# A recommendation kernel's item stage: two of 32 gathered neighbours read as SBUF columns by ScalarE and VectorE, and a limit of two gathers in flight

## The chip, the cores and the metric

One core of a Trainium2 chip. The metric is the device time of one execution in microseconds (us); lower is better. The kernel before takes 31825.53 us, the median of 10 runs that lie between 31824.42 and 31826.89.

## The reference

Two stages. The item stage makes, for each of 50,001 items, an attention over its 32 neighbours in two embeddings of width 32. The user stage gathers, for each of 16,384 users, 100 history rows of width 128 and one target row, and ends in one number a user.

```python
def _neighbor_attn(E, near_full):                 # item stage, twice: E_in, E_out
    V = E[near_full]                              # [50001, 32, 32]
    scores = einsum('nd,nkd->nk', E, V) / sqrt(32)
    w = softmax(scores, axis=-1)
    return einsum('nk,nkd->nd', w, V)
...
h = concat([E_hist[history], a_sus[history], a_inf[history]])   # [16384, 100, 128]
t = concat([E_tgt[target], a_inf[target], a_sus[target]])       # [16384, 128]
z = relu(einsum('bld,hd->blh', h * t[:, None, :], W1) + b1)
exp_A = exp(einsum('blh,h->bl', z, W2[0])) * mask
result = h * (exp_A / sum(exp_A) ** 0.5)[..., None]
s = sum(result)                                   # one number for the whole batch
pred = cosine(s * ones, t);  return sigmoid(pred)
```

## The kernel before

Both embeddings lie side by side in one DRAM table, `egeo`, with 64 floats (256 B) a row, padded to 50,048 rows.

Item stage (L93 to L164). The items are cut into 23 iterations of 17 sub-tiles of 128 items: 391 sub-tiles. An iteration loads the neighbours' numbers `nidx`, its items' own rows `own` and the left half of `row` (L101 to L107). For a sub-tile, 32 indirect DMAs (L111), one for each neighbour, gather 128 rows of 256 B into `v`, one row to a partition; they are issued by GpSimd (POOL). Pool `n_v` has five buffers, so POOL can be up to five sub-tiles ahead. Then VectorE (DVE) multiplies by the item's own row (L120), sums to scores (L127), finds the maximum (L129, L130); ScalarE (ACT) makes the exponents (L134); DVE weighs the rows (L145, two halves), sums them (L152) and scales (L153) into `row`; ACT copies a swapped version into `trow` (L160). `own` and the exponents lie in PSUM when DVE reads them. At the end of an iteration SP's queue stores `row` to `table` and `trow` to `ttab` (L163, L164).

User stage (L176 to L292). For each of 128 blocks of 128 users, one indirect DMA gathers the targets' rows `t` from `ttab` (L197), and 100 gather the histories' rows `h` of 512 B from `table` (L233), four to a tile, with 12 tiles of `h`. PE transposes them (L246), DVE multiplies by the target and makes row sums (L248, L249), PE multiplies by W1 (L255), ACT applies the ReLU (L257), PE makes the scores (L265). Stages of three groups are interleaved. The user stage begins after the item stage's tables are stored.

The order of the instructions on each engine is the scheduler's; it also places the semaphore waits. Every indirect DMA tells of its landing by one of eight semaphores, taken in turn. At the start, ACT's queue issues a copy of 12.5 MB from `etgt` into `ttab` (L91, L92).

Of the kernel before, what the change touches and what calls it, by code (L numbers as in the profile page):

```python
# [9 lines left out]

F32 = mybir.dt.float32
I32 = mybir.dt.int32
AF = mybir.ActivationFunctionType
ALU = mybir.AluOpType
AX = mybir.AxisListType

P = 128
ITEMS = 50001
K = 32
G = 32  # L20
DE = 64
D = 128
# [7 lines left out]
NSUB = 17  # L30
NITER = -(-ITEMS // (P * NSUB))
ROWS = NITER * P * NSUB

# [7 lines left out]
def kernel(  # L43
# [11 lines left out]
    out: bass.AP,  # L55
):
    nc = tc.nc

    const = ctx.enter_context(tc.tile_pool(name="const", bufs=1))
    dram = ctx.enter_context(tc.tile_pool(name="dram", bufs=1, space=bass.MemoryType.DRAM))  # L60


    table = dram.tile([ROWS, D], F32, name="table")

    ttab = dram.tile([ROWS, D], F32, name="ttab")

    ident = const.tile([P, P], F32, name="ident")
# [16 lines left out]
    scale = 1.0 / math.sqrt(G)  # L84
    near_v = near.rearrange("(i p j) k -> i p j k", p=P, j=NSUB)
    egeo_v = egeo.rearrange("(i p j) d -> i p j d", p=P, j=NSUB)
    ehist_v = ehist.rearrange("(i p j) d -> i p j d", p=P, j=NSUB)
    table_v = table.rearrange("(i p j) d -> i p j d", p=P, j=NSUB)
    ttab_v = ttab.rearrange("(i p j) d -> i p j d", p=P, j=NSUB)

    nc.scalar.dma_start(ttab[0 : ITEMS - 1, 0:DE], etgt[0 : ITEMS - 1, :])  # L91
    nc.scalar.dma_start(ttab[ITEMS - 1 : ITEMS, 0:DE], etgt[ITEMS - 1 : ITEMS, :])  # L92
    with (  # L93
        tc.tile_pool(name="n_in", bufs=2) as n_in,
        tc.tile_pool(name="n_v", bufs=5) as n_v,
        tc.tile_pool(name="n_p", bufs=2) as n_p,
        tc.tile_pool(name="n_s", bufs=3) as n_s,
        tc.tile_pool(name="n_ps", bufs=2, space=bass.MemoryType.PSUM) as n_ps,
    ):
        for it in range(NITER):  # L100
            nidx = n_in.tile([P, NSUB, K], I32, name="nidx")  # L101
            nc.sync.dma_start(nidx, near_v[it])
            own = n_in.tile([P, NSUB, 2 * G], F32, name="own")
            nc.sync.dma_start(own, egeo_v[it])
            row = n_in.tile([P, NSUB, D], F32, name="row")
            nc.sync.dma_start(row[:, :, 0:DE], ehist_v[it])
            trow = n_in.tile([P, NSUB, 2 * G], F32, name="trow")  # L107
            for j in range(NSUB):
                v = n_v.tile([P, K, 2, G], F32, name="v")
                for k in range(K):  # L110
                    nc.gpsimd.indirect_dma_start(  # L111
                        out=v[:, k].rearrange("p t d -> p (t d)"),
                        out_offset=None,
                        in_=egeo,
                        in_offset=bass.IndirectOffsetOnAxis(ap=nidx[:, j, k : k + 1], axis=0),
                    )
                own_ps = n_ps.tile([P, 1, 2 * G], F32, name="own_ps")
                nc.scalar.copy(own_ps[:, 0, :], own[:, j, :])  # L118
                prod = n_p.tile([P, K, 2, G], F32, name="prod")
                nc.vector.tensor_tensor(  # L120
                    prod.rearrange("p k t d -> p k (t d)"),
                    v.rearrange("p k t d -> p k (t d)"),
                    own_ps.to_broadcast([P, K, 2 * G]),
                    ALU.mult,
                )
                sc = n_s.tile([P, 2, K], F32, name="sc")
                nc.vector.tensor_reduce(sc.rearrange("p t k -> p k t"), prod, AX.X, ALU.add)  # L127
                top = n_s.tile([P, 2], F32, name="top")
                nc.vector.tensor_reduce(top, sc, AX.X, ALU.max)  # L129
                nc.vector.tensor_scalar(top, top, -scale, None, ALU.mult)  # L130
                ex = n_ps.tile([P, 2, K], F32, name="ex")
                tot = n_s.tile([P, 2, 1], F32, name="tot")
                for t in range(2):
                    nc.scalar.activation(  # L134
                        ex[:, t, :],
                        sc[:, t, :],
                        AF.Exp,
                        bias=top[:, t : t + 1],
                        scale=scale,
                        accum_out=tot[:, t, :],  # L140
                    )
                nc.vector.reciprocal(tot, tot)  # L142
                wv = n_p.tile([P, 2, G, K], F32, name="wv")
                for t in range(2):
                    nc.vector.tensor_tensor(  # L145
                        wv[:, t].rearrange("p d k -> p k d"),
                        v[:, :, t, :],
                        ex[:, t, :].rearrange("p (k o) -> p k o", o=1).to_broadcast([P, K, G]),
                        ALU.mult,
                    )  # L150
                att = n_s.tile([P, 2, G], F32, name="att")
                nc.vector.tensor_reduce(att, wv, AX.X, ALU.add)  # L152
                nc.vector.tensor_tensor(  # L153
                    row[:, j, DE:D].rearrange("p (t d) -> p t d", t=2),
                    att,
                    tot.to_broadcast([P, 2, G]),
                    ALU.mult,
                )
                for t in range(2):
                    nc.scalar.copy(  # L160
                        trow[:, j, t * G : (t + 1) * G], row[:, j, D - (t + 1) * G : D - t * G]
                    )
            nc.sync.dma_start(table_v[it], row)  # L163
            nc.sync.dma_start(ttab_v[it][:, :, DE:D], trow)  # L164


    num = const.tile([P, UC], F32, name="num")
# [3 lines left out]
    hist_v = history.rearrange("(p i j) l -> i p j l", p=P, j=BSUB)  # L171
    tidx = const.tile([P, UC], I32, name="tidx")
    nc.scalar.dma_start(tidx, target.rearrange("(p c) -> p c", p=P))
    tidf = const.tile([P, UC], F32, name="tidf")
    nc.vector.tensor_copy(tidf, tidx)
    with (  # L176
# [12 lines left out]
        def target_rows(c):  # L189

            if c % BSUB == 0:
                hidx = u_in.tile([P, BSUB, L], I32, name="hidx")
                nc.sync.dma_start(hidx, hist_v[c // BSUB])
                hists[c // BSUB] = hidx

            t = u_t.tile([P, D], F32, name="t")
            nc.gpsimd.indirect_dma_start(  # L197
                out=t,
                out_offset=None,
                in_=ttab[0:ITEMS, :],  # L200
                in_offset=bass.IndirectOffsetOnAxis(ap=tidx[:, c : c + 1], axis=0),
            )
            users[c] = {"t": t, "hidx": hists[c // BSUB][:, c % BSUB, :]}

        def target_work(c):
# [8 lines left out]
            junk = u_t.tile([P, D], F32, name="junk")  # L214
            nc.scalar.activation(junk, t, AF.Square, accum_out=tsq[:, c : c + 1])
            idf = u_s.tile([P, L], F32, name="idf")
# [11 lines left out]
        def gather(c, g):  # L228
            u = users[c]
            h = u_h.tile([P, LG, D], F32, name="h")  # L230
            for q in range(LG):
                l = g * LG + q
                nc.gpsimd.indirect_dma_start(  # L233
                    out=h[:, q, :],
                    out_offset=None,
                    in_=table,
                    in_offset=bass.IndirectOffsetOnAxis(ap=u["hidx"][:, l : l + 1], axis=0),
                )
            u["h", g] = h

        def turn(c, g):
            u = users[c]
            h = u.pop(("h", g))
            hT_ps = ps_t.tile([P, LG, P], F32, name="hT_ps")
            for q in range(LG):
                nc.tensor.transpose(hT_ps[:, q, :], h[:, q, :], ident)  # L246
            xT = u_x.tile([D, LG, P], F32, name="xT")
            nc.vector.tensor_tensor(xT, hT_ps, u["tT"].to_broadcast([D, LG, P]), ALU.mult)  # L248
            nc.vector.tensor_reduce(u["hsum"][:, g * LG : (g + 1) * LG], h, AX.X, ALU.add)  # L249
            u["xT"][g] = xT  # L250

        def hidden(c, g):
# [3 lines left out]
            z = u_x.tile([HID, LG, P], F32, name="z")  # L256
            nc.scalar.activation(z, z_ps, AF.Relu, bias=b1_sb)  # L257
            u["z"][g] = z

        def scored(c, g):  # L260
# [9 lines left out]
            ea = u_s.tile([P, L], F32, name="ea")  # L270
            nc.scalar.activation(ea, u["score"], AF.Exp)
            nc.vector.tensor_tensor(ea, ea, u["keep"], ALU.mult)
# [7 lines left out]
        for s in range(len(groups) + 2):  # L280
            if s < len(groups):
                c, g = groups[s]
# [12 lines left out]
    with (  # L295
# [3 lines left out]
        root = f_s.tile([P, UC], F32, name="root")  # L299
        nc.scalar.activation(root, den, AF.Sqrt)  # L300
        part = f_s.tile([P, UC], F32, name="part")
# [6 lines left out]
        s = f_s.tile([P, 1], F32, name="s")  # L308
# [4 lines left out]
        nc.vector.tensor_scalar(n1, n1, float(D), EPS * EPS, ALU.mult, ALU.max)  # L313
        nc.scalar.activation(n1, n1, AF.Sqrt)
        n2 = f_s.tile([P, UC], F32, name="n2")
# [65 lines left out]
```

## Time and profile before

| what | value |
|---|---|
| median of 10 runs | 31825.53 us |
| the profiled execution | 31823.54 us, its span 31821.7 us |
| POOL busy | 24022.8 us (75%), 25446 instructions |
| PE busy | 15251.9 us (48%) |
| DVE busy | 8950.1 us (28%) |
| ACT busy | 2850.7 us (9%) |
| gathers of the item stage (L111) | 12512, 944 ns each |
| gathers of the user stage (L233, L197) | 12800 and 128, 944 ns each |
| first gather of the item stage, of the user stage | at 8.4 us, at 15654.1 us |

The page gives, for an engine, the time in which its instructions ran. Under the groups, each line has the busy time of a group, the mean of one instruction in ns, and the idle time of the engine just before these instructions with what ended it. "issue" means that the engine waited for nothing that the profile shows. An indirect DMA on POOL counts as busy while POOL makes its descriptors; the transfer itself goes on afterwards, and "landing" is the moment at which its semaphore is complete, counted from the instruction's start. The chain of waits follows the work that ended last back through what released it; each of its pieces has a start, a length and a name.

### The profile page before, as it was taken

Reading aid. Unit: us, or ns where it says so; the run is one execution under the profiler, and the core shown is the slowest. Engines: PE = TensorE matmul, PEld = TensorE weight load, DVE = VectorE, ACT = ScalarE, POOL = GpSimd, SP = SyncE. Lnnn points to the kernel's source line nnn. Section 1 sums busy time; section 2 is a strip of 40 time slices with the busy share of each in tenths; the row PEclk is TensorE's granted clock in tenths of the full one; section 3 lists DMA queues with packets and bytes.
Section 4 is the critical chain, followed back from the end, with each engine's and each line's share of the span. In section 5 each row is a group of like instructions: output and inputs, shape, how many; then the busy total and the mean of one; then the engine's idle time right before and its main releaser. Section 6 shows DMA issues by size and latency. Waiting matters only on the chain.

```text
span 31821.7 us, 154035 instructions
## 1 busy us (share of the span) xinstructions
PE 15251.9 (48%) x44931; PEld 9633.2 (30%) x44931; DVE 8950.1 (28%) x10957; ACT 2850.7 (9%) x6458; POOL 24022.8 (75%) x25446
## 2 busy tenths in 40 slices
PE   0000000000000000000299999999999999999999
PEld 0000000000000000000155555555555555555555
DVE  2222222222222222222222222222222222222222
ACT  0000000000000000000011111111111111111111
POOL 7777777777777777777777777777777777777777
PEclk9999999999999999999955555555555555555555
DMA  2111111111111111111122222222222222222221
GB/s 50 30 30 30 30 31 33 30 30 30 30 34 30 30 30 30 31 33 28 37 54 53 54 53 54 53 54 54 53 54 53 54 53 54 54 53 54 53 54 52
DMA packets 981065, 1358.75 MB, mean 43 GB/s; under 512 B 559873, under 2 KB 564353, under 8 KB 977281
## 3 DMA queue, kind: packets, MB, share of 16 engines
q0 software_dynamic: 814080, 1258.87, 17.0%
q1 hardware_dynamic: 115952, 77.16, 0.9%
q10 hardware_dynamic: 50192, 12.87, 0.2%
q8 instruction: 363, 5.95, 0.1%
q14 instruction: 478, 3.91, 0.0%
HBM read 1308.76 MB, written 51.30 MB: 43 GB/s over the span
## 4 chain that ended last, share of the span: by engine, by line
POOL 48%; issue 19%; PE 16%; DMA 13%; DVE 2%; ACT 1%; POOLq 0%; ACTq 0%; SPq 0%; DVEq 0%
POOL v L111 35%; POOL h L233 13%; DMA h<-table,hidx 11%; PE z_ps L255 8%; PE score L265 5%; PE hT_ps L246 3%; DMA v<-in_egeo_dram,nidx 2%; DVE xT L248 2%; ACT z L257 1%; POOL t L197 0%; POOLq L233 0%; DVE ea L274 0%; DVE tT L211 0%; DMA ttab<-trow 0%; DMA nidx<-in_near_dram 0%
## 5 line engine op out<-in xcount | busy, mean ns | idle before, releaser
L233 POOL DMA_INDIRECT h<-table,hidx x12800 | 12088.6, 944 | 3899.7 <-issue 3169.8
L111 POOL DMA_INDIRECT v<-in_egeo_dram,nidx x12512 | 11812.7, 944 | 3818.2 <-issue 3727.6
L209 PE MATMUL hT_ps<-ident,t 128*128 128x128 f32 x128 | 53.9, 421 | 15650.1 <-DMA t<-ttab,tidx 15650.1
L265 PEld LDWEIGHTS score<-w_sb,z 128*128 128x128 f32 x25600 | 6226.6, 334 | 1075.0 <-ACT z L257 1068.7
L255 PE MATMUL z_ps<-xT,w1T 128*128 128x512 f32 x6400 | 6529.5, 1124 | 0.0
L265 PE MATMUL score<-w_sb,z 128*128 128x1 f32 x25600 | 5906.4, 335 | 228.7 <-ACT z L257 150.7
L246 PE MATMUL hT_ps<-ident,h 128*128 128x128 f32 x12800 | 4724.1, 440 | 675.3 <-DMA h<-table,hidx 523.0
L249 DVE TENSOR_REDUCE hsum<-h 128x4 f32<-128x512 f32 x3200 | 2194.3, 686 | 9256.4 <-DMA h<-table,hidx 9239.4
L209 PEld LDWEIGHTS hT_ps<-ident,t 128*128 128x128 f32 x128 | 28.7, 224 | 15650.3 <-ACT idf L217 15650.3
L246 PEld LDWEIGHTS hT_ps<-ident,h 128*128 128x128 f32 x12800 | 2675.4, 209 | 5447.2 <-issue 3254.6
L120 DVE TENSOR_TENSOR prod<-v,own_ps 128x2048 f32<-128x2048 f32 x391 | 894.2, 2287 | 10800.5 <-DMA v<-in_egeo_dram,nidx 10800.2
L257 ACT ACTIVATE z<-z_ps,b_sb 128x512 f32<-128x512 f32 x3200 | 2198.7, 687 | 13456.8 <-PE z_ps L255 13345.8
L248 DVE TENSOR_TENSOR xT<-hT_ps,tT 128x512 f32<-128x512 f32 x3200 | 2209.7, 691 | 2026.7 <-PE hT_ps L246 2025.4
L255 PEld LDWEIGHTS z_ps<-xT,w1T 128*128 128x128 f32 x6400 | 1746.2, 333 | 0.0
L145 DVE TENSOR_TENSOR wv<-v,ex 128x1024 f32<-128x1024 f32 x782 | 1399.2, 1868 | 0.0
L118 ACT COPY own_ps<-own 128x64 f32<-128x64 f32 x391 | 84.4, 216 | 11505.2 <-DVE prod L120 11503.8
L127 DVE TENSOR_REDUCE sc<-prod 128x64 f32<-128x2048 f32 x391 | 894.5, 2288 | 13.5
L152 DVE TENSOR_REDUCE att<-wv 128x64 f32<-128x2048 f32 x391 | 893.7, 2286 | 13.4
L160 ACT COPY trow<-row 128x32 f32<-128x32 f32 x782 | 131.7, 215 | 2466.0 <-DVE row L153 2466.0
L134 ACT ACTIVATE ex<-sc,top 128x32 f32<-128x32 f32 x782 | 227.7, 291 | 1082.6 <-DVE top L130 1070.0
L142 DVE RECIPROCAL tot<-tot 128x2 f32<-128x2 f32 x391 | 64.8, 166 | 362.4 <-ACT ex L134 362.4
L197 POOL DMA_INDIRECT t<-ttab,tidx x128 | 120.8, 944 | 60.6 <-issue 60.6
(49 smaller groups left out, 808.9 us busy)
## 6 DMA issues: line engine op xcount, KB each, us to landing
h<-table,hidx POOLq DMA_INDIRECT x12800, 2.5
v<-in_egeo_dram,nidx POOLq DMA_INDIRECT x12512, 2.4
table<-row SPq DMA_DIRECT2D x23, 1088.0 KB, 4.4
own<-in_egeo_dram SPq DMA_DIRECT2D x23, 544.0 KB, 3.7
row<-in_ehist_dram SPq DMA_DIRECT2D x23, 544.0 KB, 6.8
ttab<-trow SPq DMA_DIRECT2D x23, 544.0 KB, 6.7
ttab<-in_etgt_dram ACTq DMA_DIRECT2D x1, 12500.0 KB, 52.2
hidx<-in_history_dram SPq DMA_DIRECT2D x32, 200.0 KB, 2.5
```

What stands on the lines that cost most here:

```text
L111: nc.gpsimd.indirect_dma_start(out=v[:, k].rearrange("p t d -> p (t d)"), out_offset=None, in_=egeo, in_offset=bass.IndirectOffsetOnAxis(a ...
L120: nc.vector.tensor_tensor(prod.rearrange("p k t d -> p k (t d)"), v.rearrange("p k t d -> p k (t d)"), own_ps.to_broadcast([P, K, 2 * G]), ...
L127: nc.vector.tensor_reduce(sc.rearrange("p t k -> p k t"), prod, AX.X, ALU.add)
L145: nc.vector.tensor_tensor(wv[:, t].rearrange("p d k -> p k d"), v[:, :, t, :], ex[:, t, :].rearrange("p (k o) -> p k o", o=1).to_broadcast ...
L152: nc.vector.tensor_reduce(att, wv, AX.X, ALU.add)
L233: nc.gpsimd.indirect_dma_start(out=h[:, q, :], out_offset=None, in_=table, in_offset=bass.IndirectOffsetOnAxis(ap=u["hidx"][:, l : l + 1], ...
L246: nc.tensor.transpose(hT_ps[:, q, :], h[:, q, :], ident)
L248: nc.vector.tensor_tensor(xT, hT_ps, u["tT"].to_broadcast([D, LG, P]), ALU.mult)
L249: nc.vector.tensor_reduce(u["hsum"][:, g * LG : (g + 1) * LG], h, AX.X, ALU.add)
L255: nc.tensor.matmul(z_ps, w1T, u["xT"].pop(g), start=True, stop=True)
L257: nc.scalar.activation(z, z_ps, AF.Relu, bias=b1_sb)
L265: nc.tensor.matmul(u["score"][:, l : l + 1], z[:, q, :], w2_sb, start=True, stop=True)
```

## The change

Three things change.

First, the item stage takes two of each item's 32 neighbours out of the gathers. At the start the whole table `egeo` is brought into SBUF in transposed form, `geoT`: 128 partitions by 25,024 columns of 4 bytes, where a column holds the 128 floats of two neighbouring rows (an even and an odd item). It is made by 66 loads on SP's queue (`transposed`), PE transposes and ACT copies. For an iteration, `load` works out the address of the column of each item's last two neighbours on DVE and transposes these addresses into one row for each sub-tile and neighbour (`cols`). For a sub-tile, ScalarE reads one neighbour and VectorE the other: each loads 128 addresses into registers, 32 at a time, and copies 128 columns of 4 bytes on each partition, one instruction to a column, into `g` (`columns`). PE transposes `g` back (`turn`), ACT copies the even item's half into `v` (`even`), and DVE overwrites it with the odd item's half where the number is odd (`odd_half`). The option of fetching a neighbour by single-row DMAs on SP's queue is in the code and switched off (`SPNUM` is 0).

Second, the order of the item stage on PE, ACT, DVE and SP is written out by hand: step s issues the gathers and columns of sub-tile s, the products, scores and exponents of s-1, the weighing and sums of s-2 and the last copies of s-3, with the column copies spread in eight portions between them. The stores of `row` and `trow` go to ACT's queue. `n_p` has one buffer instead of two.

Third, each indirect DMA of both stages goes through `gather_rows`, which makes it wait for the landing of the indirect DMA issued two before it (`AHEAD` is 2).

```diff
+AHEAD = 2
+AUX = ("AAAA", "DDDD",)
+NAUX = len(AUX)
+SPNUM, SPDEN = 0, 1
+NREG = 32
+PAIRS = ROWS // 2
+NST = 3
...
+    geoT = nc.alloc_sbuf_tensor("geoT", (P, PAIRS), F32).ap()
...
+    def gather_rows(**kw):
+        g = nc.gpsimd.indirect_dma_start(**kw)
+        if len(issued) >= AHEAD:
+            tc.add_manual_dep(g.ins, issued[-AHEAD].ins.name, landed, reason="AHEAD")
+        issued.append(g)
...
+        tc.manual_schedule(engines={E.PE, E.Activation, E.DVE, E.SP}),
+        tc.tile_pool(name="n_st", bufs=2) as n_st,
-        tc.tile_pool(name="n_p", bufs=2) as n_p,
+        tc.tile_pool(name="n_p", bufs=1) as n_p,
+        tc.tile_pool(name="n_g", bufs=2) as n_g,
...
+        def transposed(q):
...
+            nc.sync.dma_start(
+                st[0:h, 0:n, :],
+                egeo_p[base : base + h * n, :].rearrange("(p n) d -> p n d", n=n),
+            )
...
+                for r in range(m):
+                    nc.tensor.transpose(ps[:, r, 0:h], st[0:h, n0 + r, :], ident[0:h, 0:h])
+                if (n0 // 4) % 2:
+                    nc.vector.tensor_copy(into[:, n0 : n0 + m, :], ps[:, 0:m, 0:h])
+                else:
+                    nc.scalar.copy(into[:, n0 : n0 + m, :], ps[:, 0:m, 0:h])
...
+        def gather(s):
...
+            k1 = K - NAUX - 1
+            by_sp = s * SPNUM % SPDEN < SPNUM
...
+            for k in range(k1 if by_sp else k1 + 1):
+                gather_rows(
+                    out=v[:, k].rearrange("p t d -> p (t d)"),
...
+        def columns(s, a, i0):
+            e = AUX[a][i0 // NREG]
+            vals = registers(s, a + 1, ENGINE[e], i0, geoT_at, geoT_at + 4 * (PAIRS - 1))
+            g = subs[s]["g"][a].bitcast(U8)
+            copy = nc.scalar.copy if e == "A" else nc.vector.tensor_copy
+            for i in range(i0, i0 + NREG):
+                copy(g[:, 4 * i : 4 * i + 4], geoT_b[:, ds(vals[i - i0] - geoT_at, 4)])
+
+        def turn(s):
+            back = n_pt.tile([P, 4, P], F32, name="pt")
+            for a in range(NAUX):
+                nc.tensor.transpose(back[:, a, :], subs[s]["g"][a], ident)
...
+        def even(s):
+            nc.scalar.copy(subs[s]["aux"], subs[s]["back"][:, 0:NAUX, 0 : 2 * G])
...
+        def odd_half(s):
+            nc.vector.copy_predicated(
+                subs[s]["aux"],
...
+                subs[s]["back"][:, 0:NAUX, 2 * G : 4 * G],
+            )
...
-            nc.sync.dma_start(table_v[it], row)
-            nc.sync.dma_start(ttab_v[it][:, :, DE:D], trow)
+            if j == NSUB - 1:
+                nc.scalar.dma_start(table_v[it], row)
+                nc.scalar.dma_start(ttab_v[it][:, :, DE:D], trow)
...
+        for s in range(NT + 3):
+            if s < NT:
+                if s % NSUB == NSUB // 2 and s // NSUB + 1 < NITER:
+                    load(s // NSUB + 1)
+                gather(s)
+            one, two, three = (0 <= s - d < NT for d in (1, 2, 3))
+            work = [
+                lambda: one and turn(s - 1),
+                lambda: (two and weighted(s - 2, 0), one and even(s - 1)),
+                lambda: two and weighted(s - 2, 1),
+                lambda: one and (odd_half(s - 1), products(s - 1)),
+                lambda: one and scores(s - 1),
+                lambda: two and attend(s - 2),
+                lambda: three and finish(s - 3),
+                lambda: one and exponents(s - 1),
+            ]
+            for w in range(len(work)):
+                work[w]()
+                if s < NT:
+                    for blocks in (acts, dves):
+                        n = len(blocks)
+                        for c in blocks[-(-w * n // 8) : -(-(w + 1) * n // 8)]:
+                            columns(s, *c)
...
-            nc.gpsimd.indirect_dma_start(
+            gather_rows(
                 out=t,
...
-                nc.gpsimd.indirect_dma_start(
+                gather_rows(
                     out=h[:, q, :],
```

## The prediction

> **What bounds the kernel now.** I read the page's busy times first, then its groups, then the list of waits, then the chain of waits in small windows. Busy times alone mislead here: no engine is above 75%.
>
> ```profile
> PE 15251.9 (48%) x44931; PEld 9633.2 (30%) x44931; DVE 8950.1 (28%) x10957; ACT 2850.7 (9%) x6458; POOL 24022.8 (75%) x25446
> ...
> L233 POOL DMA_INDIRECT h<-table,hidx x12800 | 12088.6, 944 | 3899.7 <-issue 3169.8
> L111 POOL DMA_INDIRECT v<-in_egeo_dram,nidx x12512 | 11812.7, 944 | 3818.2 <-issue 3727.6
> ```
>
> The two gather groups hold 23,901 us of busy time and 7,718 us of idle time that nearly all ends by itself ("issue"): together almost the whole span. The order of time shows the same as a fixed beat:
>
> ```profile
> 199.66 0.94 POOL L111 DMA_INDIRECT v<-in_egeo_dram,nidx  x1 [0.30 <-issue]
> 200.90 0.94 POOL L111 DMA_INDIRECT v<-in_egeo_dram,nidx  x1 [0.30 <-DMA v<-in_egeo_dram,nidx]
> 202.15 0.94 POOL L111 DMA_INDIRECT v<-in_egeo_dram,nidx  x1 [0.30 <-issue]
> 203.40 0.94 POOL L111 DMA_INDIRECT v<-in_egeo_dram,nidx  x1 [0.30 <-issue]
> ```
>
> A gather takes 0.945 us and the next starts 0.30 us later: one per 1.249 us (202.15 to 203.40), in both stages. The item stage is 12,512 x 1.2487 = 15,624 us, the user stage (12,800 of h, 128 of t) 12,928 x 1.249 = 16,147 us, sum 31,771; the rest of the 31,821.7 us span is 8.4 us ahead of the first gather, 22 us between the stages and the tail. The profiled execution took 31,823.5 us, 2 us under the median of 31,825.5, so I add changes to 31,824.
>
> The second thing to read is how long a gather takes to land, since the change makes gathers wait for that. From the chain of waits in three windows (start, length, what):
>
> ```profile
> 2.19 5.96 DMA nidx<-in_near_dram
> 8.15 0.28 issue
> 8.43 1.10 POOL v L111
> ...
> 198.41 2.43 DMA v<-in_egeo_dram,nidx
> 200.83 0.02 issue
> 200.86 0.02 POOLq L111
> 200.87 0.03 issue
> 200.90 0.94 POOL v L111
> ...
> 15653.36 0.04 POOLq L197
> 15653.41 0.70 issue
> 15654.11 0.94 POOL t L197
> ```
>
> An item gather lands 2.43 us after it starts (others in that view 2.33 to 2.47). In the user stage, rows of twice the size land after 2.44 to 2.59, middle 2.50. Two beats are 2.50 us. So there are already hardly more than two gathers in flight, and the new limit falls on the very moment at which the next one starts today.
>
> **The change, part by part.**
>
> *Removed gathers.* 30 of 32 neighbours stay on POOL: 391 x 2 = 782 gathers less, 782 x 1.249 = 977 us less at today's beat. All of it is on the path.
>
> *The wait.* Gather n now waits for the landing of n-2, in both stages, for all 11,730 + 12,928 = 24,658. Behind a waiting gather stand all later gathers, which are all that POOL has to do; behind them DVE and PE. If X is the time from a landing to the start of the gather that waited for it, the beat is the larger of 1.249 and (landing + X)/2. X is the number on which all hangs. Rows bound it: 0.07 (200.83 to 200.90), 0.28 (8.15 to 8.43), 0.70 (15653.41 to 15654.11). I distrust the first: the list of waits gives 274 such waits in the item stage, all with a gap of 0.30 like the 12,237 gathers that waited for nothing; a wait that truly held the gather would scatter its start with the landing (2.33 to 2.47). There the sequencer was ahead, the next gather already handed over. The other two are starts of an idle POOL, and a gather released by a landing meets an idle POOL. I take 0.28, the one gather whose own wait ended with a landing; 0.70 also follows eight semaphore instructions in a row.
> Item: (2.43 + 0.28)/2 = 1.355, x 11,730 = 15,894, against 15,624: +270 us, the saving of 977 included.
> User: (2.50 + 0.28)/2 = 1.39, x 12,928 = 17,970, against 16,147: +1,823 us. Nothing is removed here; the wait is pure cost.
>
> *Slow landings.* Today a late landing costs nothing; with the wait it does. While the 12.5 MB copy into ttab runs, gathers land after 5.8 us (median from 8 to 51 us); around the stores of an iteration (699 to 712 us) the median is 4.7. At the boundaries some five gathers lose (4.7 - 2.43)/2 = 1.1 us, 23 times: 130 us. At the start the beat is (5.8 + 0.28)/2 = 3.0 for 43 us: 14 gathers instead of 34, 27 us. Estimate 140 together, as the start overlaps the next item.
>
> *The transposed table.* 66 loads of 196 KB, 198 transposes (0.44 us), 66 ACT copies of 128x384 (0.22 at 64 wide, 0.69 at 512: about 0.55). With two staging buffers, 2.7 us for a load (nidx, 272 KB) and one copy behind another, about 2.5 us a round, 165 us; ACT begins after 51 us, as its queue is held by the ttab copy (49.4 us). So the first columns come at about 220 us and the first v buffer is free two steps later, near 285. POOL fills five buffers (150 gathers) by about 240. Stall about 50 us, once. Sum so far 190 beside the two stages.
>
> *ScalarE's and VectorE's columns, hidden or not.* A sub-tile lasts 30 x 1.355 = 40.7 us on POOL. VectorE has 11.3 us of work today (2.29 + 2.29 + 3.58 + 2.29 and four of about 0.2), one predicated copy (0.3) and 128 small copies: 0.09 each if they follow as closely as the scaling after the 128x2 reciprocal (95.87 to 95.96), 0.166 if they last like it: 11.5 to 21.2. ScalarE has 1.8 us and 128 copies at 0.125 (two trow copies in 0.34) to 0.215: 16 to 27.5. Each also loads 128 registers, which no row shows: from a semaphore instruction of the sequencer (0.017) to a whole small VectorE instruction (0.166), 2 to 21 us. VectorE 25 to 54, ScalarE 20 to 50. I take the lower half, below 40.7, and cost it at nothing: POOL's gathers hide it. If VectorE were at 54, the item stage would be 391 x 54 = 21,114. The drain after the last gather grows by two sub-steps, some 10 us. Moving the stores of row and trow from SP's to ACT's queue is 46 issues of 0.3 to 0.6 us on an engine with slack: nothing.
>
> A rule of the Trainium skill speaks against the registers: "Runtime: NRT & Kernel Launch", section on instruction fetch, gives about 200 ns for each register that a sequencer loads, even in bulk. No row here shows a register load. By that rule 128 loads are 25.6 us, VectorE's step is an estimated 48.7 us, the item stage 19,040 and the whole 37,250.
>
> Second, does VectorE slow the gathers? Gathers are 940/945 ns (min/median) in a stretch with VectorE 28% busy, and the same in the user stage: not today. "SBUF — State Buffer", section "Who interferes with whom", says that a VectorE copy with both ends in SBUF can take the port pair that GpSimd needs and block it for a whole instruction; today's large operations are not of that kind, the 128 new copies may be. By it up to 128 x 0.166 = 21 us of a sub-tile could be blocked; no run here shows it, and I leave it out.
>
> Sum: 31,824 + 270 + 1,823 + 190 = 34,107: I say 34,100.
>
> **Rivals.**
> *Faster: the wait costs nothing.* If the sequencer passes a landing on within 0.07, as that row reads, item is 1.25 x 11,730 = 14,663 (-961), user 1.285 x 12,928 = 16,612 (+465); with 190 for start and slow landings 31,520. If it is hidden wholly, -977 + 190 gives 31,040. It decides at X = 0.09, where the two stages cancel. For it: the 200.90 row. Against: 0.30 in every one of them. That the limit isn't in force at all (no wait in the program) ends in the same place.
> *Slower by little: X = 0.12*, the time from a landing to VectorE's start (the last gather 87.26, landing 2.43 later, prod at 89.81): item 1.275 (-668), user 1.31 (+789), 190: 32,140.
> *Slower by much: the columns bind, or X is 0.70.* VectorE passes POOL's 40.7 us when a register costs over 0.137 us at the small spacing. At 54 us: 31,824 + 5,490 + 1,823 + 190 = 39,330. X = 0.70 gives item 1.565 (+2,733), user 1.60 (+4,538): 39,290. For it: nothing here shows a register load, and the one other idle start is long.
>
> **How the numbers follow.** X from 0.2 to 0.4 with the columns hidden, 0.47: 33,100 to 35,600, centre 34,100. Little slower, 0.14. Much slower, 0.20. Faster, 0.19 (31,000 to 31,700). A measurement here can tell 0.2% (64 us) from no change; only a narrow X near 0.09 falls within: 0.03, taken from faster and little slower. So faster 0.17, same 0.03, slower 0.80. The range runs from 31,000 (the free wait) to 36,500, leaving out most of the much-slower case and little else; the likeliest case's own range is 33,100 to 35,600.
>
> **What would show it.** POOL's gathers keep 945 ns, but the gap before them in both groups is put down to DMA instead of issue, with starts in pairs or a steady 1.36 (item) and 1.39 (user). Item stage about 15,900 us, user stage about 18,000. The user stage is the cleanest: only the wait changed there. Wrong: a user beat of 1.25 with gaps of 0.30 (the wait is free); a POOL that waits for v buffers released by VectorE or ScalarE (the columns bind); gathers longer than 945 ns (the port).

## The result and the profile after

The kernel after takes 36,628.68 us (median of 8 runs, 36,614.93 to 36,654.23), beside 31,825.83 us for the kernel before in the same comparison: 1.151 times as long, with a 95% interval of 1.150 to 1.152. The prediction was 34,100 us; the sign was right, the loss was 2.1 times the forecast (4,803 us instead of 2,274), and the time lies 129 us above the range.

The profiled execution took 36,628.49 us, its span 36,626.4. From the starts of the gathers in its trace: the first starts at 9.6 us, the item stage takes 16,506 us (11,730 gathers, 1.407 us each), 23 us lie between the stages, the user stage takes 20,069 us (12,928 gathers, 1.552 us each), the tail 18 us.

The page of the kernel after: busy time of each engine, then the shares of the chain that ended last, then four groups of instructions.

```profile
PE 16229.4 (44%) x45932; PEld 9562.5 (26%) x45932; DVE 12711.4 (35%) x61557; ACT 7855.2 (21%) x56963; POOL 23270.6 (64%) x24664
...
DMA 69%; issue 12%; PE 12%; DVE 2%; POOL 2%; ACT 2%; POOLq 0%; ACTq 0%; DVEq 0%; SPq 0%
...
L84 POOL DMA_INDIRECT h<-table,hidx x12800 | 12079.4, 944 | 7729.1 <-DMA h<-table,hidx 5736.1
L84 POOL DMA_INDIRECT v<-in_egeo_dram,nidx x11730 | 11069.8, 944 | 5444.9 <-DMA v<-in_egeo_dram,nidx 4876.0
...
L240 ACT COPY g<-geoT 128x4 uint8 x50048 | 4919.1, 189 | 2151.1 <-issue 2149.8
...
L240 DVE COPY g<-geoT 128x4 uint8 x50048 | 3847.7, 195 | 2252.8 <-issue 2135.3
```

A gather still holds POOL for 944 ns. What grew is the idle time before it: 5,444.9 us for `v` and 7,729.1 for `h`, where it was 3,818.2 and 3,899.7, and most of it now ends with a landing and not by itself. The chain is 69% DMA. VectorE and ScalarE carry 100,096 column copies, and neither stands in the chain with more than 2%.

In the order of time POOL's beat of 0.30 us gaps is gone. Start, length, instruction, and in brackets the gap before it with what ended it, in the user stage of the kernel after:

```profile
16749.07 0.94 POOL L84 DMA_INDIRECT h<-table,hidx  x1 [0.31 <-issue]
16750.69 0.95 POOL L84 DMA_INDIRECT h<-table,hidx  x1 [0.68 <-DMA h<-table,hidx]
16751.94 0.94 POOL L84 DMA_INDIRECT h<-table,hidx  x1 [0.30 <-DMA h<-table,hidx]
16753.92 0.94 POOL L84 DMA_INDIRECT h<-table,hidx  x1 [1.04 <-DMA h<-table,hidx]
16755.17 0.94 POOL L84 DMA_INDIRECT h<-table,hidx  x1 [0.31 <-issue]
```

Gathers now start in pairs, and the gaps ahead of the pairs differ: 0.68, then 1.04. The chain of waits around the same moment (start, length, what) tells the two apart:

```profile
16747.06 0.02 issue
16747.08 0.04 POOLq L84
16747.12 0.70 issue
16747.82 2.61 DMA h<-table,hidx
16750.43 0.26 issue
16750.69 2.47 DMA h<-table,hidx
16753.15 0.02 issue
16753.18 0.04 POOLq L84
16753.22 0.70 issue
16753.92 2.54 DMA h<-table,hidx
```

From a landing to the start of the gather that waited for it there are two prices, not one. Where the gather itself holds the wait it is 0.26 us (16750.43 to 16750.69). Where POOL's sequencer has a semaphore instruction ahead of the gather ("POOLq") it is 0.02 + 0.04 + 0.70 = 0.76 us (16753.15 to 16753.92). Over the whole trace the first is 0.259 us with hardly any scatter (least 0.258), the second 0.763 in the user stage, with 9 of 10 of the gathers that had to wait between 0.760 and 0.766. A tile that PE or VectorE gives back late would scatter it. Where two semaphore instructions stand ahead of a gather (39 times) the middle is 0.824, so the price goes with the instructions.

In the item stage the first price is the rule, with a third one now and then. The chain in a window there:

```profile
355.96 2.45 DMA v<-in_egeo_dram,nidx
358.41 0.26 issue
358.67 2.50 DMA v<-in_egeo_dram,nidx
361.17 1.74 issue
362.90 2.48 DMA v<-in_egeo_dram,nidx
```

The 1.74 us (358.67 + 2.50 to 362.90) returns at every 106th gather in the order of the program. It is plainest where every gather waits (e4 below): of the 233 gathers in that place, 201 started 1.73 to 1.74 us after the landing and 31, with a semaphore instruction ahead of them, some 3.34 us.

How often does a semaphore instruction stand ahead of a gather? The view of the gathers' line counts them (duration in ns, first and last start). The kernel after, user stage from 17,000 us on:

```profile
L84 POOLq EVENT_SEMAPHORE  x3280: 17/43/43, 17000.2 to 36596.3; - x193
```

and the kernel before, whole:

```profile
L233 POOLq EVENT_SEMAPHORE  x3219: 17/43/43, 15709.3 to 31790.0; - x190
```

About one for four gathers, in both: a tile of `h` holds four gathers, and the first of them waits for the tile to be free as well as for a landing. Before, it costs nothing: of 25,439 gaps between gathers only two are over 0.4 us, since the sequencer hands a gather over while POOL still works on the one before. After, 13,130 of 24,657 gaps are.

### The profile page after: what moved, and what is told of

It reads as the page before. It is cut to its first block, busy times and chain, and to the rows that moved or that the text cites. A ratio compares the mean times of both kernels' runs of the same rounds, so it can differ in the third digit from the quotient of the medians.

```text
span 36626.4 us, 262157 instructions
## 1 busy us (share of the span) xinstructions
PE 16229.4 (44%) x45932; PEld 9562.5 (26%) x45932; DVE 12711.4 (35%) x61557; ACT 7855.2 (21%) x56963; POOL 23270.6 (64%) x24664
## 4 chain that ended last, share of the span: by engine, by line
DMA 69%; issue 12%; PE 12%; DVE 2%; POOL 2%; ACT 2%; POOLq 0%; ACTq 0%; DVEq 0%; SPq 0%
DMA v<-in_egeo_dram,nidx 38%; DMA h<-table,hidx 31%; PE z_ps L461 6%; PE score L471 5%; DVE xT L454 2%; ACT z L463 2%; POOL v L84 2%; PE hT_ps L452 1%; POOL h L84 1%; DMA t<-ttab,tidx 0%; DVE hsum L455 0%; POOLq L84 0%; DVE ea L478 0%; ACT ea L477 0%; DVE den L479 0%
## 5 line engine op out<-in xcount | busy, mean ns | idle before, releaser
L84 POOL DMA_INDIRECT h<-table,hidx x12800 | 12079.4, 944 | 7729.1 <-DMA h<-table,hidx 5736.1
L84 POOL DMA_INDIRECT v<-in_egeo_dram,nidx x11730 | 11069.8, 944 | 5444.9 <-DMA v<-in_egeo_dram,nidx 4876.0
L461 PE MATMUL z_ps<-xT,w1T 128*128 128x512 f32 x6400 | 6451.9, 1112 | 1603.9 <-DVE xT L454 1599.4
L245 PE MATMUL pt<-ident,g 128*128 128x128 f32 x782 | 363.7, 471 | 15041.0 <-DVE g L240 9864.5
L471 PEld LDWEIGHTS score<-w_sb,z 128*128 128x128 f32 x25600 | 5715.2, 328 | 1617.6 <-ACT z L463 1550.5
L452 PE MATMUL hT_ps<-ident,h 128*128 128x128 f32 x12800 | 4963.6, 440 | 1931.0 <-DMA h<-table,hidx 1915.7
L240 ACT COPY g<-geoT 128x4 uint8 x50048 | 4919.1, 189 | 2151.1 <-issue 2149.8
L452 PEld LDWEIGHTS hT_ps<-ident,h 128*128 128x128 f32 x12800 | 2984.7, 246 | 6698.3 <-DMA h<-table,hidx 3734.5
L240 DVE COPY g<-geoT 128x4 uint8 x50048 | 3847.7, 195 | 2252.8 <-issue 2135.3
L245 PEld LDWEIGHTS pt<-ident,g 128*128 128x128 f32 x782 | 141.7, 183 | 15259.0 <-DVE g L240 9972.3
L251 ACT COPY v<-pt 128x128 f32<-128x128 f32 x391 | 104.0, 266 | 2487.0 <-PE pt L245 2475.8
```

Of the source, the lines that this page charges most:

```text
L84: g = nc.gpsimd.indirect_dma_start(**kw)
L240: copy(g[:, 4 * i : 4 * i + 4], geoT_b[:, ds(vals[i - i0] - geoT_at, 4)])
L461: nc.tensor.matmul(z_ps, w1T, u["xT"].pop(g), start=True, stop=True)
L471: nc.tensor.matmul(u["score"][:, l : l + 1], z[:, q, :], w2_sb, start=True, stop=True)
```

## The experiments

The runs were made in three batches, on the chips numbered 3, 0 and 2; which one the result came from is not on record. So each stands beside the kernel before on its own chip, which took 36,292 us in the first batch (seven runs, 36,284 to 36,298) and 31,809 us in the second and third. Where the landings can be read there, their medians are a little shorter (2.37 us item, 2.46 us user, beside 2.44 and 2.52 in the kernel after's first trace).

### First batch: no limit, the limit alone, three, one

**e1_no_limit.** The columns without the limit.

```diff
-AHEAD = 2
+AHEAD = 10**9
```

> The changed kernel with AHEAD at 10**9, so that no gather waits for an earlier one; the columns stay. Theory (the wait is the whole loss: a gather released by a landing starts 0.26 us after it, because the sequencer can no longer hand it over early; the columns are hidden): both stages fall back to one gather per 1.249 us. Item stage 11,730 x 1.249 = 14,650 us and up to 60 us of a late start, user stage 16,150, the whole 30,850 to 30,950: faster than before by 2.8%. Rival A (the columns on ScalarE and VectorE hold POOL back, by late buffers or by the port that VectorE and POOL share): the item stage stays above 15,624, gathers longer than 945 ns or waits of POOL for v buffers, the whole above 31,825. Rival B (the user stage suffers from something else in the change): its beat stays above 1.30, the whole above 32,000.

Measured: 38,956.76 us, ratio 1.073 (1.072 to 1.075) against 36,292. If the limit alone were the cause, this kernel would have been faster than the one before; here it is slower. Page groups of this kernel:

```profile
L84 POOL DMA_INDIRECT v<-in_egeo_dram,nidx x11730 | 11100.0, 946 | 8974.5 <-DVE wv L305 5505.7
L84 POOL DMA_INDIRECT h<-table,hidx x12800 | 12107.6, 946 | 6433.5 <-issue 3584.7
L240 ACT COPY g<-geoT 128x4 uint8 x50048 | 5869.5, 190 | 11021.0 <-issue 10783.9
...
L240 DVE COPY g<-geoT 128x4 uint8 x50048 | 4609.3, 184 | 8173.8 <-issue 7933.6
```

POOL waited for VectorE to release `v`, once a sub-tile, and the column copies were slow not in themselves (184 and 190 ns) but in the time between them. VectorE in order of time:

```profile
8042.48 0.17 DVE L240 COPY g<-geoT 128x4 uint8 x1 [1.22 <-issue]
8043.88 0.17 DVE L240 COPY g<-geoT 128x4 uint8 x1 [1.23 <-issue]
```

1.40 us from copy to copy, put down to nothing that the profile shows. The kernel before was 14% slower on this chip as well. So this run says something about the chip and nothing yet about the limit; it was made again below.

**e2_limit_alone.** The kernel before, with all three indirect DMAs through the same `gather_rows`; no columns.

```diff
-                nc.gpsimd.indirect_dma_start(
+                gather_rows(
```

> The kernel before with the limit of two gathers in flight alone; no columns. Theory: item beat as in the changed kernel, 1.41, x 12,512 = 17,640; user beat 1.552, x 12,928 = 20,070; with 55 for start, gap and end 37,760, some 1,130 over the changed kernel, which is the 782 gathers more at 1.41 and little else. Rival A (part of the changed kernel's item beat comes from the columns): an item beat nearer 1.35, the item stage 16,900, the whole about 37,000.

Measured: 36,799.14 us, ratio 1.014 (1.012 to 1.016): little beside this chip's slow kernel before, but the beats are those of the limit, item 1.362 us and user 1.523 us. With the limit this chip gives the user stage almost the time of the kernel after (19,685 us here). The time is nearer to rival A (about 37,000 us) than to the theory (37,760). Landings 0.06 us shorter than those of the result take 0.03 us off the theory's beats. That brings the user beat to 1.52, as measured, and the item beat from 1.41 to 1.38, that of the kernel after in its later run (e9: 1.379). The 1.362 measured lies 0.017 us lower, some 200 us of the kernel after's item stage. So under the limit the columns may cost that much; as e2 and e9 ran on different chips, it is not shown.

**e3_three.** Three in flight instead of two.

```diff
-AHEAD = 2
+AHEAD = 3
```

> The changed kernel with AHEAD at 3. Theory: a gather waits for a landing that lies 2.44 + 0.26 = 2.70 us (item) after a start three beats, 3.75 us, earlier: over a microsecond of slack, so it is handed over early again. Only the rare long delays (every 106th gather starts 1.74 us after its landing instead of 0.26; slow landings) can still show: beats 1.249 to 1.275, item 14,650 to 14,950, user 16,150 to 16,480, the whole 30,900 to 31,500. Rival C (the wait costs its quarter of a microsecond in every gather, however early the landing): beat 1.249 + 0.26 = 1.51 in both stages, the whole near 37,000.

Measured: 39,131.83 us, ratio 1.078 (1.076 to 1.080): the same disturbance as in e1 (item beat 1.706 us, e1 1.711). No verdict on the limit.

**e4_one.** One in flight: every gather waits for the one before it.

```diff
-AHEAD = 2
+AHEAD = 1
```

> The changed kernel with AHEAD at 1: each gather waits for the one before it, so the beat is landing plus X with nothing beside it. Theory: item 2.436 + 0.26, plus 0.50 in one of 30 and 1.48 in one of 106, plus slow landings, 2.75 to 2.78; user 2.52 + 0.26 plus 0.50 in one of four and 1.48 in one of 106, 2.92 to 2.96. The item stage 32,400, the user stage 38,000, the whole 70,000 to 71,000. Rival (the landing itself gets shorter when no other gather is in flight): landing below 2.3 and the beats below 2.6.

Measured: 68,834.19 us (one run), item beat 2.679 us, user beat 2.890 us. The chain of waits of this kernel:

```profile
40002.13 0.26 issue
40002.39 2.55 DMA h<-table,hidx
40004.94 0.26 issue
40005.20 2.52 DMA h<-table,hidx
```

With one gather in flight there is nothing to overlap, so the prices can be added up. Item: landing 2.368, plus 0.259, plus 0.50/30 for the semaphore instruction that stands ahead of one gather in a sub-tile, plus 1.48/106, gives 2.66. User: 2.463 + 0.259 + 0.50/4 + 0.014 = 2.86. Both are within about 1% of the measurement. The expectation was a little too long because its landings were those of the result. They do not get shorter with one in flight, as the rival had it: 2.368 and 2.463 here, 2.366 and 2.463 in the kernel before of the next batch.

### Second batch: the limit taken away, in all or in the user stage alone; larger tiles

**e5_before_again.** The kernel before with no edit, for its landings and beats.

> The kernel before itself, with a profile. In the first four runs it took 36,292 us beside them, not 31,826 as it did when the change was measured. Theory D (the chip decides: on that chip gathers that run into one another land late, and everything that goes through the DMA rings waits): where the time is near 31,826, gathers land after 2.43 and 2.50 us; where it is near 36,290, POOL has gaps behind buffers that its readers give back late, and landings far over 2.5 us. Rival (the 31,826 belonged to an earlier state of every chip): no chip gives it again.

Measured: 31,809.09 us (one run), 1.248 us a gather in both stages, landing medians 2.37 and 2.46 us. It gives the kernel before no trace where it takes 36,292 us, so that half of the expectation was not tried.

**e6_no_limit_again.** The kernel of e1, with the same edit.

> The changed kernel without the limit, once more. On a chip where the kernel before takes 31,826, theory (the wait is the whole loss) says 30,850 to 30,950, both stages at one gather per 1.249 us. Rival A (the columns hold POOL back): above 31,825 with an item stage above 15,624. On a chip where the kernel before takes 36,290 it gives 38,950 as it did, from the item stage (20,070 us, POOL waiting 13.8 us in each sub-tile for VectorE).

Measured: 30,857.77 us, ratio 0.970 (0.968 to 0.972). The page's groups and, below, a line of the waits (what waited for what: us, times, longest):

```profile
L84 POOL DMA_INDIRECT h<-table,hidx x12800 | 12078.4, 944 | 3900.8 <-issue 3076.3
L84 POOL DMA_INDIRECT v<-in_egeo_dram,nidx x11730 | 11071.8, 944 | 3602.5 <-issue 3471.8
```

```profile
POOL v L84 <- DVE wv L305: 20.2, 1, 20.2
```

Beats 1.250 and 1.248 us, as before. The columns wholly hide: apart from one stall of 20.2 us at the start, POOL never waits for an engine that carries them. The gain of 951 us is 782 gathers at 1.249 us (977), less about that stall. So the whole loss of the change comes with the limit.

**e7_item_limit.** The limit in the item stage only.

```diff
-        if len(issued) >= AHEAD:
+        if len(issued) >= AHEAD and kw["in_"] is egeo:
```

> The changed kernel with the limit in the item stage alone. Where the kernel before takes 31,826: theory says item stage as in the changed kernel (16,510 us), user stage back at 12,928 x 1.249 = 16,150, the whole 32,710, so that 3,920 of the 4,803 us come from the user stage's wait. Rival B (the user stage suffers from something else in the change): its beat stays above 1.30.

Measured: 32,352.73 us, ratio 1.017 (1.015 to 1.020). The item beat is 1.377 us (16,156 us), the user beat 1.248 us again. Against e6 the limit in the item stage costs 1,495 us. The expectation, worked with the landings of the result's chip, was 357 us too long; each landing here is 0.07 us shorter, which over two in flight is 0.035 x 11,730 = 411 us.

**e8_eight.** One tile of `h` for eight gathers, and half as many tiles, so that one gather in eight instead of four stands behind a semaphore instruction.

```diff
-        tc.tile_pool(name="u_h", bufs=12)
+        tc.tile_pool(name="u_h", bufs=6)
...
-            h = u_h.tile([P, LG, D], F32, name="h")
+            n = c * NG + g
+            if n % 2 == 0:
+                both["h"] = u_h.tile([P, 2, LG, D], F32, name="h")
+            h = both["h"][:, n % 2]
```

> The changed kernel with tiles of h for eight gathers and six of them, instead of four and twelve: the same rows in flight, half as many releases. Theory E (a gather with a semaphore instruction ahead of it starts 0.76 us after the landing instead of 0.26; today that is one of four in the user stage): now one of eight, user beat 1.552 to 1.487 when the waits are stepped through, user stage 20,070 to 19,230, the whole 840 us less than the changed kernel. Rival F (the fourth gather starts late because its tile is released late by PE and VectorE, not because of the instruction): fewer and larger tiles are released no earlier, the user beat stays at 1.55 or rises.

Measured: 35,575.29 us, ratio 1.118 (1.116 to 1.121); user beat 1.495 us. Against the kernel after in its later run (e9, 35,933 us) it moves the right way, but by 358 us where 840 were expected. The list of waits of this kernel has why:

```profile
POOL h L84 <- DMA h<-table,hidx: 4487.5, 9279, 2.6
POOL h L84 <- PE hT_ps L456: 979.9, 727, 2.1
```

For the larger tiles POOL waited 979.9 us for PE's transposes to release one (117.7 us in the kernel after). The starts agree: summed over the user stage, gathers behind a semaphore instruction started some 540 us later than 0.765 us after the landing they waited for, in e9 some 130 (both scaled up from the gathers whose landing the trace gives). The 410 us between them are 0.032 us a gather. So this run mixes two causes and alone is a weak witness.

### Third batch: the kernel after again, smaller tiles, three again, three neighbours

**e9_after_again.** The kernel after, no edit.

> The changed kernel itself, on the chip of this call. Where the kernel before takes 31,809 (gathers land after 2.37 and 2.46 us there, 0.06 sooner than on the chip of the result), the waits stepped through give an item beat of 1.38 (16,170 us, as in the two limited runs of the last four) and a user beat of 1.52 (19,660): the whole 35,880. Where the kernel before takes 36,290 the limit keeps the rings short: user beat 1.524 as with the limit alone, item 1.36, the whole 35,700 to 36,000, below the kernel without a limit there (38,957).

Measured: 35,932.82 us, ratio 1.130 (1.127 to 1.132); item beat 1.379 us, user beat 1.526 us. That is 696 us less than the result's 36,628.68; 0.06 us shorter landings would give 0.03 x 24,658 = 740 us. Against e7, on a chip where the kernel before takes the same time, the limit in the user stage costs 3,580 us.

**e10_two.** The opposite of e8: tiles of two gathers, so that every second one stands behind a semaphore instruction (VectorE's row sums in two instructions).

```diff
-        tc.tile_pool(name="u_h", bufs=12)
+        tc.tile_pool(name="u_h", bufs=24)
...
-            h = u_h.tile([P, LG, D], F32, name="h")
+            hs = [u_h.tile([P, 2, D], F32, name="h") for _ in range(2)]
```

> The changed kernel with two tiles of h for two gathers each instead of one for four (24 buffers instead of 12; VectorE makes the row sums in two instructions). Theory E (a semaphore instruction ahead of a gather costs 0.50 us after the landing): one of two gathers now has it, user beat about 1.64 on a chip where h lands after 2.46 us (1.52 with one of four, 1.495 measured with one of eight), the user stage 21,200, some 1,500 above the changed kernel's on the same chip. Rival F (late releases): smaller tiles are released sooner, the beat falls or stays at 1.52.

Measured: 37,480.32 us, ratio 1.178 (1.176 to 1.181): 1,548 us over e9, the item stage unchanged. The price says a quarter more of the gathers at 0.50 us: 0.125 x 12,928 = 1,616. POOL in order of time:

```profile
25000.95 0.94 POOL L84 DMA_INDIRECT h<-table,hidx  x1 [0.30 <-issue]
25002.92 0.94 POOL L84 DMA_INDIRECT h<-table,hidx  x1 [1.03 <-PE hT_ps L452]
25004.17 0.94 POOL L84 DMA_INDIRECT h<-table,hidx  x1 [0.30 <-issue]
25006.15 0.94 POOL L84 DMA_INDIRECT h<-table,hidx  x1 [1.03 <-DMA h<-table,hidx]
```

Every second gap is 1.03 us now. The releaser changes from line to line, the gap doesn't: a gather behind a semaphore instruction has two waits, for a landing and for a free tile, and the profile names the one that came last.

**e11_three_ahead.** The kernel of e3.

> The changed kernel with AHEAD at 3. Where the kernel before takes 31,809: theory, a landing 2.46 + 0.26 after the start and 3.75 us to go, so beats of 1.249 to 1.27, the whole 30,860 to 31,250. Rival C (the wait costs a quarter of a microsecond in every gather, however early the landing): beat 1.51 in both stages, near 37,000. Where the kernel before takes 36,290 it gives 39,130 as it did.

Measured: 31,164.38 us, ratio 0.980 (0.979 to 0.982), 1% over e6; beats 1.263 and 1.265 us. With three in flight a landing and the dearer price (2.46 + 0.76 = 3.22 us) fit into three beats (3.75 us); only 463 of 24,657 gaps are over 0.4 us, together 347 us longer than 0.305 each. That is about the whole difference to e6, and 232 of the 463 are the 106th gathers. So a wait on an earlier gather isn't dear in itself; it is dear when it ends after POOL has run dry.

**e12_three_neighbours.** No limit, and a third neighbour as columns, one quarter of it on VectorE and three on ScalarE.

```diff
-AHEAD = 2
-AUX = ("AAAA", "DDDD",)
+AHEAD = 10**9
+AUX = ("AAAA", "DDDD", "AADA")
```

> No limit, and three neighbours instead of two as columns: ScalarE 7 of 12 blocks of 32 columns, VectorE 5. Where the kernel before takes 31,809: POOL has 391 gathers less, 488 us, 30,370; the columns stay hidden if ScalarE's step (20 us with four blocks, some 33 with seven) and VectorE's (27, some 31 with five) stay below 29 x 1.249 = 36.2 us. Rival (ScalarE binds): above 30,858, with POOL waiting for v buffers. Where the kernel before takes 36,290 it is slower than that, as the kernel with two neighbours and no limit was.

Measured: 30,399.49 us, ratio 0.956 (0.954 to 0.957), faster than both kernels: 11,339 gathers at 1.253 us in the item stage, 12,928 at 1.248 in the user stage, and one stall of 49.3 us at the start.

## Why the prediction was right in sign and short in size

**What held.** The limit is the loss, and without it the columns are free: e6 without the limit gains 3.0% and e9 with it loses 13.0%, each against 31,809 us. The 0.07 row was rightly distrusted, since no gather started less than 0.258 us after the landing it waited for; the rival in which the wait costs nothing falls. Its price for a wait that is wholly hidden, 31,040 us, is close to what e6 took with no wait at all. The columns stayed hidden, with a start stall of 20.2 us in e6 where 50 were allowed. The register loads, which no row had shown, are now in the trace of the kernel after (least, median and longest time in ns, first and last start):

```profile
L200 DVEq TENSOR_LOAD <-cols x1564: 2097/2145/2353, 56.7 to 16488.9; - x196
L200 ACTq TENSOR_LOAD <-cols x1564: 1944/1977/5552, 172.0 to 16460.9; - x196
```

A load of 32 registers takes 1.98 us on ScalarE and 2.15 us on VectorE, 62 and 67 ns a register, and a sub-tile's four loads 7.9 and 8.6 us, in the lower half of the bounds taken (2 to 21 us). Part of a load runs beside the engine's earlier work: the gaps before ScalarE's columns are 2,149.8 us in all, 1.37 us a load.

"Runtime: NRT & Kernel Launch" of the Trainium skill, under "Instruction fetch mechanics", gives about 200 ns a register. Its "Terms" speak of loads from HBM; these come from the tile `cols` in SBUF, and for them the measurement decides, at 62 and 67 ns. The rule of "SBUF — State Buffer", under "Who interferes with whom", that a VectorE copy can shut GpSimd out, does not show here: with 128 copies of four bytes in a sub-tile the gathers keep 944 ns. Whether copies of this form are of the kind the rule means, no run here shows.

**What failed: the step "I take 0.28" for X, used for every gather.** For three of four gathers of the user stage it was right within 0.02 us (0.259). For the fourth it is 0.763. The step had that row in hand (0.04 POOLq, 0.70 issue) and made it a price for all gathers in a rival, at 39,290 us, instead of asking which gathers have a semaphore instruction ahead of them; the view of line L233, shown above, says 3,219, one in four. In the kernel after a group of four holds two landings on its slower side, one of each price: 2 x 2.52 + 0.26 + 0.76 = 6.06 us, 1.515 a gather. From the rows of before alone, 2 x 2.50 + 0.28 + 0.76 = 6.04 us, 1.51, would have made the user stage 19,521 us instead of 17,970, and the whole about 35,660 us, within the range.

Of the 2,521 us by which the profiled execution (36,628) exceeds the sum (34,107), the user stage has 2,099 and the item stage, with the 190 us for the start and slow landings counted to it, 422. Of the user stage's 2,099, the step from 1.39 to 1.515 is 0.125 x 12,928 = 1,616. The rest of the beat, 0.037 us or some 480 us, is only estimated: the 106th gather 1.48/106 = 0.014 us (180 us), late landings 0.014 (their mean is 0.028 us over the median, halved by two in flight, 180 us), and some 120 us that I put down to two chains of landings of which the later one counts. The item stage's excess has the same parts, and one semaphore instruction in a sub-tile (386 x 0.50 = 193 us at most).

The user beat against the share of gathers behind a semaphore instruction, on the chips of the second and third batch, is the test of this step. "Worked out" is (landings of 2.46 + 0.26 + 0.50 where it applies) for the slower side of the pairs:

| share | kernel | worked out, us | measured, us |
|---|---|---|---|
| no limit | e6 | 1.249 | 1.248 |
| one in eight | e8 | 1.42 | 1.495 (0.032 of it by tiles released late) |
| one in four | e9 | 1.485 | 1.526 |
| one in two | e10 | 1.61 | 1.646 |

From one in four to one in two the measured step is 0.120 us where 0.125 was worked out. All three kernels with a limit lie about 0.04 us above what was worked out, once e8's late tiles are taken off; on the result's chip it was 0.037, the rest of the beat estimated above.

**The range.** Its top, 36,500, was set to leave the dear row out, because as a price for all gathers it led to 39,290. Mixing cases that are both true at once, by counting, would have put it higher.

**What stays open.** Why the kernel before took 36,292 us in the first batch, and why 0.7 or 1.4 us lie there between column copies that elsewhere follow every 0.071 (VectorE) or 0.095 us (ScalarE), is not shown: there is no trace of the kernel before from that batch, and whether the chip or the occasion made it slow was not tried. Under a limit of two or one the disturbance is not seen there: e2's 1.523 us is the limit's own beat, and in e4, with the columns, the copies follow every 0.071 and 0.095 us again. With three or no limit it is (e3, e1). The kernel after did not run in that batch; from e2's beats it would take some 1.362 x 11,730 + 19,685 + 55 = 35,720 us, which would be less than 36,292. That is an estimate and no run. What recurs at every 106th gather is not known either; it goes by gathers, since in e10, with nearly twice as many semaphore instructions, it stays at every 106th.

## What to carry to other kernels

When an engine that never stopped is made to wait, price the restart by its kinds: count in the trace of before how many of the instructions have a semaphore instruction of the sequencer ahead of them, and take for those the row in which such an instruction met an idle engine. Prices that hide behind an engine that is always busy come out all at once when a limit lets it run dry. A limit on transfers in flight was nearly free here where the landing and the restart fit into its beats with room to spare (three in flight, e11: 1% over e6) and dear where the landing alone just filled them (two, e9: 16% over e6).

## What the runs showed of the hardware that was not expected

A semaphore instruction of POOL's sequencer lasts 0.04 us in the user stage, yet makes the gather behind it start 0.50 us later when POOL is idle (0.763 against 0.259 us). When POOL is busy it costs nothing: in the kernel before, gathers behind one have the same gap of 0.305 us as the others. That the gather's own preparation begins only after that instruction would explain it; this was only argued. The traces show the time alone: the gather starts 0.70 us (user stage) or 0.72 us (item stage) after the end of the instruction that held the landing.

Every 106th indirect DMA started 1.48 us later than the others when POOL was waiting (2.58 us where it stood behind a semaphore instruction), and without the limit none of this was seen (in e6 two gaps of 24,657 are over 0.4 us).

The same program took 31,809 us on chips 0 and 2, 36,292 us on chip 3 and 31,826 us beside the result, with at most 0.2% between the runs of one batch.

The granted TensorE clock did not set the time: in the result's runs of the kernel after it was 0.73 in one of 36,627 us and 0.89 in one of 36,630.
